# The second stage of a conv block as one fixed order of instructions, with its layer norm by transposes, bn_stats and Newton steps

## The chip, the cores and the metric

The kernel runs on one core of a Trainium2 chip. The metric is the time of one execution on the device in microseconds (us), the median over several runs. A program on one core has no second die to compare with, so a run counts as fast where it is not over 1.5% above the fastest of the same kernel. Only such runs are compared.

The engines are named as in the profile: PE (matrix products), PEld (loads of its weights, which overlap PE), DVE (vector), ACT (activation functions), POOL (general), SP (issues transfers).

## What the kernel computes

The input is sixteen images of 192 channels and 64 x 64 pixels. The part that the change touches is the second half of the block, after the batch norm's statistics are known.

```
mixed = gelu(batchnorm(mixed))                     # mixed: gated result of the first stage, in DRAM
x  = x + conv1x1(mixed, out_proj_w, out_proj_b)    # 192 -> 192
h2 = (x - mean_c(x)) / sqrt(var_c(x) + 1e-6)       # layer norm over the 192 channels (then ln2_w, ln2_b)
m  = gelu(conv1x1(h2, fc1_w, fc1_b))               # 192 -> 768
x  = x + conv1x1(m, fc2_w, fc2_b)                  # 768 -> 192
# then a depthwise 3x3 convolution whose kernel depends on the image; a mask leaves 4 taps
t    = relu(gamma * (mean_pixels(x) @ w1.T - running_mean) * rsqrt(running_var + 1e-5) + beta)
taps = (t @ w2.T + b2) * mask
out  = depthwise_conv(x, taps) + bias
```

All data is 32-bit floating point.

Of the kernel before, what the change touches and what calls it, by code (L numbers as in the profile page):

```python
"""A conv block (layer norm, gated directional scan, batch norm, MLP) followed by a
pooled dynamic depthwise convolution, on one core.

Layout. Images are taken in pairs (A, B). The 192 channels of a pair fill three tiles of 128
partitions: tile 0 is A's channels 0-127, tile 1 is B's channels 0-127, tile 2 holds channels
128-191 of A on partitions 0-63 and those of B on partitions 64-127. Per-channel constants
have two classes: class 0 for tiles 0 and 1, class 1 for tile 2.

Phase 1, per pair: layer norm, input projection, depthwise conv, four scans, local conv, gate;
the gated result goes to DRAM, its batch statistics stay on chip.  # L10
Phase 2, per pair: batch norm, gelu, output projection, layer norm, MLP; the image pair stays
in SBUF for the pooled dynamic convolution, and only its result is stored.
"""
# [8 lines left out]
F32 = mybir.dt.float32  # L22
AF = mybir.ActivationFunctionType
# [4 lines left out]
C = 192          # channels  # L28
HW = 64          # rows and columns of an image
NPIX = HW * HW  # L30
RW = HW + 2      # a padded row
CH = 512         # pixels of a chunk: 8 rows, one PSUM bank
CR = CH // HW    # rows of a chunk
NCH = NPIX // CH
GR = 2 * CR      # rows of a group of two chunks
NG = HW // GR
NFC = 6          # blocks of 128 hidden channels
LNG = 4          # chunks that share one pass of the layer norm's square root
RED = 48
NTAP = 4         # taps that the mask of the dynamic kernel lets through  # L40

# columns of the packed per-channel constants
# [6 lines left out]
def conv_block_kernel(ctx: ExitStack, tc: tile.TileContext, x, prm, w_in, w_out, w_fc1, b_fc1, w_fc2, w1, bn1, w2, out):  # L49
# [8 lines left out]
    def tiles_of(src, p, lo, hi):  # L58
        """The pieces of a pair's pixels lo..hi in DRAM: tile, partitions, source."""
        a, b = 2 * p, 2 * p + 1  # L60
        return (
            (0, slice(0, 128), src[a, 0:128, lo:hi]),
            (1, slice(0, 128), src[b, 0:128, lo:hi]),
            (2, slice(0, 64), src[a, 128:C, lo:hi]),
            (2, slice(64, 128), src[b, 128:C, lo:hi]),
        )

    def load_cls(dst, src):
        """A [192, n] array as its two classes of partitions."""
        nc.sync.dma_start(dst[:, 0], src[0:128])  # L70
        nc.sync.dma_start(dst[0:64, 1], src[128:C])
        nc.sync.dma_start(dst[64:128, 1], src[128:C])

    def pair_matmul(t, ps, w, bd, col, rhs):
        """ps = (weights' columns col.. of tile t)^T @ (the pair's 192 channels).

        w: [128, 2, n] weights by class of input channel; bd: [128, 128] its corner of class 1
        to class 1, block diagonal."""
# [10 lines left out]
    # ---------------------------------------------------------------- constants  # L89
# [14 lines left out]
    # x - mean over the channels as a matrix product  # L104
# [13 lines left out]
    def fold(w, col):  # L118
        """Scales a weight's rows (input channels) by a layer norm's weight."""
        for cls in range(2):  # L120
            nc.vector.tensor_scalar_mul(w[:, cls], w[:, cls], vec(cls, col))

    def corner(pool, name, w, col):
        """The block diagonal of a weight's class 1 inputs to its class 1 outputs."""
# [6 lines left out]
    def center(ps_tag, pool, rhs):  # L131
        """The three tiles of x - mean, in PSUM."""
# [7 lines left out]
    # ================================================================ phase 1  # L140
# [3 lines left out]
    with ExitStack() as phase:  # L144
# [4 lines left out]
        # biases of the two projections with the layer norm's bias in them  # L149
# [18 lines left out]
        # decays, and the factor mix * (1 - decay) * scale of each direction  # L168
# [21 lines left out]
        # the directions' factors as diagonals, to sum the scans in PSUM  # L190
        diag = k1.tile([128, 2, 4, 128], F32, tag="diag", name="diag")
        # the decays along padded rows, zero on the padding, where the state starts anew
# [9 lines left out]
        # the variances of LNG chunks go to 2*LNG rows of one bank; and back from there  # L202
# [13 lines left out]
        # images with a border of zeros, and the vertical scans  # L216
# [13 lines left out]
        for p in range(n_pairs):  # L230
            # ---- layer norm without its affine part
# [26 lines left out]
            for t in range(3):  # L258
                cls = t // 2
                # ---- projection and depthwise conv  # L260
# [15 lines left out]
                # ---- scans down and up, row by row  # L276
# [10 lines left out]
                # ---- scans along the rows, local conv, gate  # L287
# [33 lines left out]
        # ---- batch norm as a scale and a bias per channel  # L321
# [3 lines left out]
        # class 1: the two halves of the partitions have half of the images each  # L325
# [21 lines left out]
    # ================================================================ phase 2  # L347
# [28 lines left out]
    fold(wf1, LN2W)  # L376

    # the pair's images, with a row of zeros above and columns of zeros beside
# [7 lines left out]
    op = ctx.enter_context(tc.tile_pool(name="o2", bufs=2))  # L386
    ps2 = ctx.enter_context(tc.tile_pool(name="ps2", bufs=2, space=PSUM))

    for p in range(n_pairs):
        xi = ximg[p % n_img]  # L390
        sums = wp.tile([128, 3, NCH], F32, tag="sums", name="sums")
        for c in range(NCH):
            lo, hi = c * CH, (c + 1) * CH
            x2 = lp.tile([128, 3, CH], F32, tag="x2", name="x2")
            for t, q, src in tiles_of(xv, p, lo, hi):
                nc.sync.dma_start(x2[q, t], src)
            mx = lp.tile([128, 3, CH], F32, tag="mx2", name="mx2")
            nc.sync.dma_start(mx, mixed_d[p, :, :, lo:hi])

            # ---- batch norm, gelu, output projection, residual  # L400
            for t in range(3):
                cls = t // 2
                nc.scalar.activation(mx[:, t], mx[:, t], AF.Gelu, bias=bn_bi[:, cls:cls + 1], scale=bn_sc[:, cls:cls + 1])
            for t in range(3):
                ps = ps2.tile([128, CH], F32, tag="a", name="ps_o", bufs=3)
                pair_matmul(t, ps, wo, wo_bd, 0, lambda tt, q, mx=mx: mx[q, tt])
                nc.vector.scalar_tensor_tensor(x2[:, t], ps, vec(t // 2, OUTB), x2[:, t], ALU.add, ALU.add)  # L407

            # ---- layer norm without its affine part
            xc = center("a", ps2, lambda tt, q, x2=x2: x2[q, tt])  # L410
            sq = wp.tile([128, 3, CH], F32, tag="sq2", name="sq2", bufs=1)
            for t in range(3):
                nc.scalar.activation(sq[:, t], xc[t], AF.Square)
            h = wp.tile([128, 3, CH], F32, tag="h2", name="h2")
            rstd = []
            for i in range(2):
                q = slice(64 * i, 64 * i + 64)
                pw = ps2.tile([128, CH], F32, tag="f1", name="ps_v", bufs=2)
                nc.tensor.matmul(pw, mean_w, sq[:, i], start=True, stop=False)
                nc.tensor.matmul(pw, mean_w[q], sq[q, 2], start=False, stop=True)  # L420
                rs = wp.tile([128, CH], F32, tag="rs2", name="rs2")
                nc.scalar.activation(rs, pw, AF.Sqrt, bias=eps6)  # L422
                nc.vector.reciprocal(rs, rs)  # L423
                nc.vector.tensor_mul(h[:, i], xc[i], rs)  # L424
                nc.vector.tensor_mul(h[q, 2], xc[2][q], rs[q])

            # ---- MLP: the second product trails the first by one block of hidden channels
            po = [ps2.tile([128, CH], F32, tag="f2", name="ps_f2", bufs=3) for _ in range(3)]

            def second(m, gl, po=po):  # L430
                st, sp = m == 0, m == NFC - 1
                for i in range(2):
                    nc.tensor.matmul(po[i], wf2[:, m, 0:128], gl[:, i], start=st, stop=sp)  # L433
                for i in range(2):
                    nc.tensor.matmul(po[2][64 * i:64 * i + 64], wf2[:, m, 128:C], gl[:, i], start=st, stop=sp)  # L435

            last = None
            for m in range(NFC):
                cols = slice(128 * m, 128 * m + 128)
                gl = wp.tile([128, 2, CH], F32, tag="gl", name="gl", bufs=3)  # L440
                pf = [ps2.tile([128, CH], F32, tag="f1", name="ps_f1", bufs=2) for _ in range(2)]
                for i in range(2):
                    nc.tensor.matmul(pf[i], wf1[:, 0, cols], h[:, i], start=True, stop=False)  # L443
                for i in range(2):
                    q = slice(64 * i, 64 * i + 64)
                    nc.tensor.matmul(pf[i], wf1[q, 1, cols], h[q, 2], start=False, stop=True)  # L446
                for i in range(2):
                    nc.scalar.activation(gl[:, i], pf[i], AF.Gelu, bias=bf1[:, m:m + 1])  # L448
                if last is not None:
                    second(m - 1, last)  # L450
                last = gl
            second(NFC - 1, last)
# [85 lines left out]
```

## The kernel before

Images are taken in pairs A and B. A pair's channels fill three tiles of 128 partitions: tile 0 has A's channels 0-127, tile 1 has B's, and tile 2 has channels 128-191 of A on its lower and of B on its upper 64 partitions. The first stage (layer norm, projection, convolutions, scans, gate) is not touched. The second stage goes through the 8 pairs, and through each pair in 8 chunks of 512 pixels, 64 chunks in all. The 768 hidden channels of the MLP are 6 blocks of 128.

A product over a pair's 192 channels is split in this way, and each such product changes the shape in which PE's array is used:

```
def pair_matmul(t, ps, w, bd, col, rhs):
    if t < 2:
        hi = slice(64 * t, 64 * t + 64)
        nc.tensor.matmul(ps, w[:, 0, col:col + 128], rhs(t, slice(0, 128)), start=True, stop=False)   # "full", 128x128
        nc.tensor.matmul(ps, w[hi, 1, col:col + 128], rhs(2, hi), start=False, stop=True)             # "half", 64 rows
    else:
        nc.tensor.matmul(ps, bd, rhs(2, slice(0, 128)), start=True, stop=False)                       # block diagonal
        for i in range(2):                                                                            # "columns", 64 columns
            nc.tensor.matmul(ps[64*i:64*i+64], w[:, 0, col+128:col+C], rhs(i, slice(0, 128)), start=False, stop=True)
```

The second stage of one chunk was written straight on:

```
# ---- batch norm, gelu, output projection, residual
for t in range(3):
    nc.scalar.activation(mx[:, t], mx[:, t], AF.Gelu, bias=..., scale=...)
for t in range(3):
    ps = ps2.tile([128, CH], F32, tag="a", name="ps_o", bufs=3)
    pair_matmul(t, ps, wo, wo_bd, 0, ...)
    nc.vector.scalar_tensor_tensor(x2[:, t], ps, vec(t // 2, OUTB), x2[:, t], ALU.add, ALU.add)
# ---- layer norm without its affine part
xc = center("a", ps2, lambda tt, q, x2=x2: x2[q, tt])          # x - mean as a matrix product, 3 tiles in PSUM
for t in range(3):
    nc.scalar.activation(sq[:, t], xc[t], AF.Square)
for i in range(2):
    q = slice(64 * i, 64 * i + 64)
    pw = ps2.tile([128, CH], F32, tag="f1", name="ps_v", bufs=2)
    nc.tensor.matmul(pw, mean_w, sq[:, i], start=True, stop=False)       # variance, on all 128 partitions
    nc.tensor.matmul(pw, mean_w[q], sq[q, 2], start=False, stop=True)
    nc.scalar.activation(rs, pw, AF.Sqrt, bias=eps6)
    nc.vector.reciprocal(rs, rs)                                         # 128 x 512
    nc.vector.tensor_mul(h[:, i], xc[i], rs)
    nc.vector.tensor_mul(h[q, 2], xc[2][q], rs[q])
# ---- MLP: the second product trails the first by one block
for m in range(NFC):
    ... first product, full and half, for both images (pf, 2 banks)
    ... Gelu of both images
    if last is not None: second(m - 1, last)                             # full and columns
    last = gl
second(NFC - 1, last)
... results into the pair's image in SBUF, with their sums for the pooling
```

After a pair's eighth chunk came its pooling, its taps (matmuls with one moving column) and its convolution in 12 units, all before the next pair in the text of the program. A scheduler, not the text, settles in which order each engine takes the instructions.

## Time and profile before

| | before |
|---|---|
| median (3 runs) | 8107.52 us (8107.06 to 8109.49) |
| end of the first stage in the profile | 3864.6 us |
| first MLP product to last MLP result, 64 chunks | 3918.4 to 8029.6, 4111.2 us, 64.2 us a chunk |
| PE busy in that stretch | 3527.8 us, granted clock 0.89 |
| tail, last result to end | 78 us |

The page and the views that show this are read line by line in the prediction below. In short: in the second stage PE is the engine with the most work, and it idles in every chunk while the layer norm goes through ACT and DVE.

### The profile page before, as it was taken

How to read it: one execution, taken by the hardware profiler on the slowest of the kernel's cores; microseconds unless marked ns; L12 is line 12 of the kernel's file. 1: busy time of each engine (PE TensorE's matmuls, PEld its weight loads, DVE VectorE, ACT ScalarE, POOL GpSimd, SP SyncE). 2: the span in 40 equal slices, each digit the busy share in tenths (PEclk: the TensorE clock that was granted, in tenths of full speed). 3: DMA queues.
4: the chain of work that ended last, by engine and by line, in shares of the span. 5: the costliest groups of instructions: out<-in, count | busy, mean ns of one | idle time of the engine just before them, and what ended most of it. 6: DMA issues, size and time to landing. Idle time of an engine off the chain costs nothing.

```text
span 8107.6 us, 39958 instructions
## 1 busy us (share of the span) xinstructions
PE 6342.4 (78%) x13812; PEld 1932.3 (24%) x13812; DVE 4665.9 (58%) x6936; ACT 1722.3 (21%) x2473; POOL 150.8 (2%) x234
## 2 busy tenths in 40 slices
PE   8668686767768776755788888888888888888885
PEld 2222222222222222211222222222222222222221
DVE  4998989799898979999323224223242242322423
ACT  2112111112111111210222222222222222222222
POOL 0000000000000000000100000000000000000000
PEclk7787777778787777867798998988989889889897
DMA  1010101001010100000101011011010010100101
GB/s 49 11 51 11 34 21 42 18 13 50 11 34 24 39 18 13 34 11 34 31 24 47 31 31 50 28 32 46 24 55 24 28 52 30 55 24 24 55 24 35
DMA packets 113882, 256.48 MB, mean 32 GB/s; under 512 B 13792, under 2 KB 15072, under 8 KB 113680
## 3 DMA queue, kind: packets, MB, share of 16 engines
q1 hardware_dynamic: 85520, 153.25, 6.2%
q0 software_dynamic: 28160, 100.68, 3.4%
q8 instruction: 109, 1.79, 0.1%
q14 instruction: 93, 0.76, 0.0%
HBM read 153.21 MB, written 100.66 MB: 31 GB/s over the span
## 4 chain that ended last, share of the span: by engine, by line
PE 50%; DVE 34%; issue 9%; DMA 4%; ACT 4%; SPq 0%; POOL 0%; ACTq 0%; POOLq 0%; DVEq 0%
DVE mx L56 10%; PE ps_f L443 9%; PE ps_f L433 8%; DVE dimg L56 5%; PE ps_f L446 5%; DVE rs L423 4%; PE ps_f L435 4%; DVE bt L56 3%; DMA mx<-mixed_d 3%; DVE tb L56 3%; PE cmb L308 3%; DVE lr L301 2%; PE ps_cen L81 2%; PE pr L255 2%; PE ps_o L82 2%
## 5 line engine op out<-in xcount | busy, mean ns | idle before, releaser
L443 PE MATMUL ps_f<-h,wf 128*128 128x512 f32 x1536 | 880.4, 701 | 543.0 <-DVE h L424 518.3
L454 DVE SCALAR_TENSOR_TENSOR ximg<-ps_f,pv,x 128x512 f32<-128x512 f32 x192 | 144.4, 752 | 1898.3 <-PE ps_f L433 1875.4
L56 DVE SCALAR_TENSOR_TENSOR dimg<-pimg,pv,dimg 128x1024 f32<-128x1024 f32 x768 | 946.2, 1280 | 46.7 <-ACT dimg L272 39.2
L56 DVE SCALAR_TENSOR_TENSOR mx<-dimg,pv,mx 128x1024 f32<-128x1024 f32 x768 | 957.6, 1272 | 0.9
L448 ACT ACTIVATE gl<-ps_f,bf 128x512 f32<-128x512 f32 x768 | 485.4, 683 | 1376.2 <-PE ps_f L446 1375.5
L433 PE MATMUL ps_f<-gl,wf 128*128 128x512 f32 x1536 | 761.8, 618 | 0.0
L423 DVE RECIPROCAL rs<-rs 128x512 f32<-128x512 f32 x128 | 420.3, 3325 | 507.1 <-ACT rs L422 507.1
L308 PE MATMUL cmb<-rl,diag 128*128 128x512 f32 x384 | 260.3, 767 | 419.3 <-DVE rl L302 419.3
L443 PEld LDWEIGHTS ps_f<-h,wf 128*128 128x128 f32 x1536 | 290.4, 210 | 1089.2 <-issue 991.4
L308 PE MATMUL cmb<-lr,diag 128*128 128x512 f32 x384 | 266.5, 783 | 337.0 <-DVE lr L301 263.1
L56 DVE SCALAR_TENSOR_TENSOR bt<-bt,dec,dimg 128x64 f32<-128x64 f32 x1512 | 419.9, 278 | 158.6 <-ACT bt L283 157.9
L446 PE MATMUL ps_f<-h,wf 64*128 64x512 f32 x1536 | 477.0, 701 | 0.0
L296 ACT ACTIVATE sg<-ps_g,bi 128x512 f32<-128x512 f32 x192 | 125.2, 685 | 1610.4 <-DVE mx L315 1461.9
L56 DVE SCALAR_TENSOR_TENSOR tb<-tb,dec,dimg 128x64 f32<-128x64 f32 x1512 | 422.6, 280 | 61.7 <-ACT tb L283 61.3
L435 PE MATMUL ps_f<-gl,wf 128*64 128x512 f32 x1536 | 414.2, 618 | 0.0
L56 DVE SCALAR_TENSOR_TENSOR o<-ximg,taps,o 128x1024 f32<-128x1024 f32 x288 | 357.3, 1279 | 98.4 <-ACT o L490 95.0
L407 DVE SCALAR_TENSOR_TENSOR x<-ps_o,pv,x 128x512 f32<-128x512 f32 x192 | 143.5, 751 | 419.0 <-PE ps_o L82 328.6
L433 PEld LDWEIGHTS ps_f<-gl,wf 128*128 128x128 f32 x1536 | 260.1, 189 | 482.0 <-issue 482.0
L81 PE MATMUL ps_p<-hc,wi 128*128 128x512 f32 x256 | 199.6, 872 | 112.6 <-ACT sg L296 112.6
L255 PE MATMUL pr<-rs,spread 8*128 8x512 f32 x384 | 247.0, 774 | 39.5 <-DVE rs L250 32.3
L301 DVE TENSOR_TENSOR_SCAN lr<-dtab,dimg 128x528 f32<-128x528 f32 x192 | 240.0, 1250 | 46.7 <-PE cmb L308 46.6
L264 ACT ACTIVATE pimg<-ps_p,bi 128x512 f32<-128x512 f32 x192 | 132.6, 691 | 570.2 <-PE ps_p L82 422.4
(177 smaller groups left out, 6801.4 us busy)
## 6 DMA issues: line engine op xcount, KB each, us to landing
mixed_d<-mx POOLq DMA_DIRECT2D x96, 512.0 KB, 2.9
mx<-mixed_d SPq DMA_DIRECT2D x64, 768.0 KB, 4.9
hc<-in_x_dram SPq DMA_DIRECT2D x128, 256.0 KB, 5.2
x<-in_x_dram SPq DMA_DIRECT2D x128, 256.0 KB, 3.5
out_dram<-o POOLq DMA_DIRECT2D x64, 512.0 KB, 2.9
hc<-in_x_dram SPq DMA_DIRECT2D x128, 128.0 KB, 5.2
x<-in_x_dram SPq DMA_DIRECT2D x128, 128.0 KB, 3.7
out_dram<-o POOLq DMA_DIRECT2D x64, 256.0 KB, 3.4
```

What stands on the lines that cost most here:

```text
L56: nc.vector.scalar_tensor_tensor(o, in0, scalar, in1, ALU.mult, ALU.add, **kw)
L81: nc.tensor.matmul(ps, w[:, 0, col:col + 128], rhs(t, slice(0, 128)), start=True, stop=False)
L82: nc.tensor.matmul(ps, w[hi, 1, col:col + 128], rhs(2, hi), start=False, stop=True)
L255: nc.tensor.matmul(pr, spread[:, j, t], rs, start=True, stop=True)
L301: nc.vector.tensor_tensor_scan(lr, dtab[:, cls, 0], row, 0.0, ALU.mult, ALU.add)
L308: nc.tensor.matmul(dst, diag[:, cls, k], src, start=(k == 0), stop=(k == 3))
L423: nc.vector.reciprocal(rs, rs)
L433: nc.tensor.matmul(po[i], wf2[:, m, 0:128], gl[:, i], start=st, stop=sp)
L435: nc.tensor.matmul(po[2][64 * i:64 * i + 64], wf2[:, m, 128:C], gl[:, i], start=st, stop=sp)
L443: nc.tensor.matmul(pf[i], wf1[:, 0, cols], h[:, i], start=True, stop=False)
L446: nc.tensor.matmul(pf[i], wf1[q, 1, cols], h[q, 2], start=False, stop=True)
L448: nc.scalar.activation(gl[:, i], pf[i], AF.Gelu, bias=bf1[:, m:m + 1])
```

## The change

The intent has two parts that do not depend on each other.

**The layer norm.** Each quarter of a chunk is transposed by PE so that pixels lie on the partitions. DVE's bn_stats then gives mean and variance of 192 channels in one instruction per image. The inverse root is taken on 128 x 8 numbers by DVE alone, from an integer shift as a first guess and three Newton steps, so ACT needs no Sqrt. Transposes of the broadcast result spread it back over the channels. The mean is not subtracted from the data at all: `W (x - mean) = (W - its mean over the input channels) x`, so the centring matrix goes into the MLP's first weight, once.

**The order.** The second stage is written as one fixed program, kept in the order of its text (`manual_schedule`). While the six MLP blocks of a chunk run, the next chunk's output projection, statistics and normalisation, and the last pair's convolution, are put into the blocks at fixed places, each product beside others of its own shape.

The core of the diff; "..." marks cuts, and "[before]" and "[after]" say from which kernel a passage is.

```
+        fold(wf1, LN2W)                     # [after] ln2_w into the weight, then the mean out of it
+        for j in range(2):
+            ...
+                pair_matmul(t, ps, cen, cen_bd, 0, lambda tt, q, cs=cs: wf1[q, tt // 2, cs])
+        ...                                  # copied back into wf1

-            xc = center("a", ps2, ...)       # [before]
-            ... Square, variance products, Sqrt, reciprocal, multiplies
+        def pixels(self, j):
+            pt = bank("ps_x")
+            for n, t in enumerate((0, 2, 1)):
+                nc.tensor.transpose(pt[:, 128*n:128*n+128], self.x2[:, t, cols], ident)
+        def moments(self, j):
+            for i in range(2):
+                nc.vector.bn_stats(self.stats[:, j, i], self.pt[j][:, i * C:(i + 1) * C])
+        def rstd(self):                      # 4 small instructions for the variance v, then
+            nc.vector.tensor_scalar(yi, vi, 1, None, ALU.logical_shift_right)
+            nc.vector.tensor_scalar(yi, yi, -1, 0x5f3759df, ALU.mult, ALU.add)
+            for _ in range(3):
+                nc.vector.tensor_mul(u, y, y)
+                nc.vector.scalar_tensor_tensor(u, u, -0.5, v, ALU.mult, ALU.mult)
+                nc.vector.scalar_tensor_tensor(y, u, 1.5, y, ALU.add, ALU.mult)
+        def spread(self, i):
+            for j in range(NB):
+                nc.tensor.transpose(self.pr[i][:, 128*j:128*j+128], self.y[:, n:n+1].broadcast_to([128, 128]), ident)
+        def norm(self, i):
+            nc.vector.tensor_mul(self.h[:, i], self.x2[:, i], self.pr[i])
+            nc.vector.tensor_mul(self.h[q, 2], self.x2[q, 2], self.pr[i][q])

+    with tc.manual_schedule():
+        ... front of chunk 0, bare
+        for k in range(n_chunks):
+            for m in range(NFC):
+                ... loads of chunk k+2 (m = 1); end of a convolution unit of the last pair
+                ... MLP first product, full                          (cur, block m)
+                if m == 1: nxt.out01_full()                          # next chunk, in its own shape
+                elif m == 2: nxt.out2_full()
+                elif m == 3: nxt.pixels(0), moments(0), pixels(1), moments(1)
+                elif m == 4: nxt.spread(0); nxt.norm(0)
+                second_full(*trail)                                  # block m-1
+                if m == 3: nxt.pixels(2), moments(2), pixels(3), moments(3); nxt.rstd()
+                elif m == 4: nxt.spread(1); nxt.norm(1)
+                ... MLP first product, half; Gelu; nxt.out01_half (m = 1)
+                second_cols(*trail); nxt.out2_cols (m = 2); nxt.gelu (m = 0)
+                ... begin of a convolution unit of the last pair
```

The convolution's units were halved (one chunk's rows instead of two), with four output buffers instead of two.

## The prediction

> **What bounds the kernel now.** I read the slices of the span first, to find the stages:
>
> ```profile
> PE   8668686767768776755788888888888888888885
> DVE  4998989799898979999323224223242242322423
> PEclk7787777778787777867798998988989889889897
> ```
>
> The span breaks near the middle. In the left half DVE is full (9s) and PE waits on it: that is the first stage, which the change leaves alone. In the right half PE is at 8, DVE at 2 to 3, and the granted clock dips again and again below full speed. The timeline puts the last first-stage instruction at 3864.6 us, the first second-stage matmul at 3888.1, the last result of the 64 chunks at 8029.6, and the end at 8107.6. So 8029.6 - 3888.1 = 4141.5 us go to 64 chunks, 64.7 us each. Only this part is at stake.
>
> Next, busy time in one ordinary chunk (from one RECIPROCAL to that of the next chunk; columns: window, length, busy of PE, PEld, DVE, ACT, POOL, granted clock, DMA share, GB/s):
>
> ```profile
> 4616.36:4677.91 61.55, 53.70 (x132) 16.11 (x132) 13.52 (x15) 15.23 (x23) 0.00 (x0) 0.92 0.08 26
> ```
>
> PE is busy 53.7 of 61.55 us, everything else a quarter or less: a PE-bound stage with a hole of some 8 us in each chunk. The chain of waits shows what is in the hole (start, length, what):
>
> ```profile
> 5059.99 1.91 PE ps_f L433 x4
> 5061.91 1.01 PE ps_f L435 x4
> 5062.92 1.05 PE ps_o L81 x2
> 5063.97 1.05 PE ps_o L82 x2
> ...
> 5069.28 4.83 DMA mx<-mixed_d
> ...
> 5076.85 0.52 ACT L422
> 5077.36 0.78 issue
> 5078.14 0.70 ACT rs L422
> 5078.84 0.02 issue
> 5078.86 6.56 DVE rs L423 x2
> 5085.43 0.56 DVE h L424
> 5085.98 0.14 issue
> 5086.12 3.75 PE ps_f L443 x4
> 5089.87 1.06 PE ps_f L446 x4
> ...
> 5093.04 1.98 PE ps_f L443 x4
> ```
>
> From the last output projection (5069.2) to the first MLP product (5086.1) the path runs through the load of the next gated image, which ACT needs for work queued ahead of the layer norm's; the ACT table load and Sqrt (L422); and two RECIPROCALs of 3.3 us. Meanwhile PE does the centring and variance products and then idles. The waits view says how long:
>
> ```profile
> PE ps_f L443 <- DVE h L424: 486.7, 60, 13.5
> ```
>
> that is 8.1 us per chunk. The last chain lines show a second charge: the first L443 group after the hole takes 3.75 us, the same group later 1.98.
>
> A third loss is at each pair's end. At 4388.98 us pooling begins, and the next MLP product starts at 4438.88: 50 us, where the ordinary gap from last MLP product to first is 5005.4 to 5024.9, 19.5 us. In between, DVE's convolution work (L56) stands ahead of the next RECIPROCAL. 30 us x 7 boundaries = 210 us, so 64 x 61.4 + 210 = 4140, which closes the account.
>
> **What the Trainium skill says.** "TensorE: Matmul & The Clock Gate", part 1 (What's actually happening): PE runs at half clock after about 3.4 us of idling and needs about as long to recover. The trace agrees: 3.75 against 1.98 us after the hole. "ScalarE: Activation LUTs", What ACT_TABLE_LOAD costs: some 1.28 us per table load. The trace has 1283 ns, at two functions, Sqrt and Gelu, per chunk. "VectorE: DVE Perf Modes", First, the fixed hardware budget: Reciprocal runs an iterated divide with a repeat count of 8. The trace has 3344 ns for 512 elements, against 0.65 us for a multiply of the same shape. The TensorE page, part 4 (PE-mode transpose), gives some 275 ns for a 128x128 bf16 transpose inside a kernel. The kernel before has none, so no run yet confirms it, least of all for 32-bit data.
>
> **The change, part by part.** Prices of PE work come from the chain: a lone matmul 1.05 us, two of one shape 1.91, so 0.86 for each further one and about 0.19 when the tile shape of the array changes (128x128, two 64-row halves side by side, two 64-column halves side by side). A side-by-side pair costs as one: 1.06 and 1.01.
>
> *Removed.* Centring (1.91+1.06+1.06+1.03 = 5.1 us) and variance products (4 x 1.05 = 4.2 us) of PE; Square, Sqrt and both table loads on ACT; both RECIPROCALs on DVE; the 8.1 us wait; the cold restart (3.75 - 1.91, some 1.8 us); 30 us at each boundary.
>
> *MLP.* 24 full products, 6 pairs of halves and 6 of columns are 36 units, 36 x 0.86 = 31.0. Before, each of six blocks changed shape four times (1.91+1.06+1.91+1.01 = 5.89, so 35.3 per chunk). Now the second product's full part follows the first's, and the next chunk's output projection goes into groups of its own shape, so three changes: 6 x 3 x 0.19 = 3.4. Sum 34.4.
>
> *Output projection.* 2 full, one pair, one block diagonal, one column pair: 5 x 0.86 = 4.3 with no extra shape change (before 6.3).
>
> *Added on PE.* 12 transposes to pixels and 8 to spread the result: 20 x 0.275 = 5.5 by the skill's figure. For a floor, the N=1 matmuls L475 show a pair of 128-column weight loads in 0.31 us warm, 0.155 each. If each 32-bit transpose is two instructions it could be 0.35 to 0.4. So 3.1 to 8.
>
> *Pooling.* Its small matmuls now stand in the stream of PE: about 5 us per pair by the warm rows (16 of 0.31 or 0.20, four of 0.19), 0.6 per chunk.
>
> *Beside PE.* DVE per chunk: six results and residuals at 0.75, 8 bn_stats (678 ns for 512 elements, so about 0.3 for 192), 15 tiny operations at 0.2 (rows of 0.15 to 0.17), 4 multiplies at 0.65, and 3 convolution units of 3 x 0.75: 4.5+2.4+3.0+2.6+6.8 = 19.3 us, under half of a chunk. ACT: 12 Gelu at 0.68, 3 at 0.8, 3 convolution starts at 0.75: 13 us. Both hide. The tight place is block 3 to 4: after the last pixels, PE has halves, columns and the next full group, about 1.05+1.05+1.9 = 4 us, and DVE in that time two or so bn_stats and the 15-step chain, 0.7+3.0. It just fits; I allow 0.3 us.
>
> Sum per chunk: 34.4+4.3+5.5+0.6+0.3 = 45.1, against 64.7. 64 x 45.1 = 2886 us.
>
> *Ends.* Before the loop, folding the mean into the weight adds 10 cold matmuls and four copies, about 10 us; the first chunk's front is bare (output projection about 12 us cold, transposes and statistics 6, chain 3, spread and norm 5): first MLP product at about 3925, against 3918.4 before. The tail was 78 us: 46 of DVE, the rest waits for two output buffers. Now 8 of pooling, 24 x 3 x 0.75 = 54 of DVE, and about 11 from last store to end as now: 75.
>
> Total 3925 + 2886 - 5 (the last chunk has no follower) + 75 = 6881 us.
>
> **Rivals.** (a) *Transposes cost more than thought*: two passes, or a drained array at each of the four switches. For: 32-bit data, no trace of them here. 0.4 each adds 2.5 us per chunk, 160 us: about 7040. At 0.155 each: about 6730. (b) *A new wait takes the hole's place*: DVE's strict order puts convolution work or the 15-step chain before what PE needs, and PE idles in block 4. For: the slack is under 1 us. Against: DVE is under half loaded and PE has another block to run after the norm. If the small steps take 0.3 instead of 0.2, PE idles 1 to 2 us per chunk: 6950 to 7000. If gaps also drop the clock it could reach 7150. (c) *DVE or DMA becomes the bound*: 19 of 45 us and a DMA share of 0.08 to 0.13 speak against it; loads run a whole chunk ahead. This would need 60 us per chunk to leave the time unchanged. (d) *The hole was hidden anyway*: no, PE is the engine waiting.
>
> **Range and chances.** The transpose price moves the total by -150 to +160, the wait by 0 to +120, and the ends by 15. I say 6880 us, 6710 to 7080 in 8 of 10. For less than 2% gain (7945) a chunk would have to cost 62 us: faster 0.97, same 0.02, slower 0.01.
>
> **What would show it.** Right: PE above 9 in the right half's slices, clock near full there, chunk period 43 to 47 us, no table loads and no RECIPROCAL of 128x512, the wait of the MLP's first product on h gone, DVE near 4 tenths, transposes near 0.2 to 0.35 us apart. Wrong: a PE wait on the Newton chain (y) or on banks of the transposes, or transposes well off 0.275 us.

## The result

| | before | after |
|---|---|---|
| median | 8107.33 us (8107.06 to 8109.49, 4 runs) | 6641.55 us (6638.98 to 6644.0, 4 runs) |
| ratio of the fast runs | 1 | 0.8195 (95%: 0.8184 to 0.8207) |
| end of the first stage in the profile | 3864.6 us | 3854.6 us |
| first MLP product to last MLP result | 3918.4 to 8029.6 us | 3903.9 to 6562.3 us |
| an ordinary chunk | 61.55 us | 40.80 us |
| tail | 78 us | 74.9 us |

A ratio here is worked out from the fast runs of both kernels; it is not quite the ratio of the two medians (0.8192). The change takes 18% off. The direction and the place were as predicted, and the time lies 68 us below the range of 6710 to 7080 us.

The slices of the span of the kernel after (40 equal slices, busy share or granted clock in tenths):

```profile
PE   8848678678678678677665569999999999999995
DVE  3898997998998987998999952353435353535355
PEclk8877787687787787777867779999999999999997
```

From slice 24 on PE shows nines without a dip, and so does its clock. The windows view gives the same as numbers. Its columns are window, length, then busy time (and instructions) of PE, PEld, DVE, ACT and POOL, then granted clock, DMA share and GB/s. First the second stage of the kernel before:

```profile
3918.40:8029.60 4111.20, 3527.76 (x8692) 1081.92 (x8692) 1175.36 (x1263) 1064.98 (x1476) 61.24 (x112) 0.89 0.11 35
```

and the same stage after, with one ordinary chunk below it:

```profile
3903.90:6562.30 2658.40, 2657.43 (x8567) 1031.71 (x8566) 1124.45 (x2837) 736.25 (x1125) 122.70 (x224) 0.99 0.16 53
5044.24:5085.04 40.80, 40.80 (x131) 15.55 (x131) 20.59 (x48) 12.50 (x19) 3.27 (x6) 1.00 0.21 65
```

PE is busy in 2657.43 of 2658.40 us. So of 583 us of idle time (4111.20 - 3527.76) all but 1 us went, and 870 us of PE's own busy time (3527.76 - 2657.43), 13.6 us a chunk. Of these, an estimate from the rows of both chains accounts for some 12: the centring and variance products, 9.3, less 2.3 for transposes, 1.1 and 2.0 in the MLP and the projection from fewer changes of shape, and 1.8 from the slow restart. The rest is not separated. Next to nothing is left to wait for in this stage: it is almost exactly as long as PE's work.

In an ordinary chunk the chain of waits of the kernel after is therefore a list of PE groups and nothing else. Its columns are start, length and what ran; these are the two blocks of one chunk that hold the transposes:

```profile
5044.24 1.91 PE ps_f L617 x4
5046.15 0.66 PE ps_x L459 x6
5046.81 1.72 PE ps_f L581 x4
5048.52 0.66 PE ps_x L459 x6
5049.18 1.06 PE ps_f L652 x4
5050.24 1.01 PE ps_f L585 x4
5051.25 1.91 PE ps_f L617 x4
5053.16 0.56 PE ps_r L491 x4
5053.72 1.72 PE ps_f L581 x4
5055.44 0.44 PE ps_r L491 x4
```

L617 and L652 are the full and half part of the MLP's first product, L581 and L585 the full part and the columns of the second. L459 are the transposes to pixels and L491 those that spread the result. Two products show as x4, so a 32-bit product is two instructions; six transposes show as x6, so a transpose is one. The instructions of a chunk's transposes take 0.66 + 0.66 + 0.56 + 0.44 = 2.32 us of PE's stream, where the prediction had 5.5. The L617 group takes 1.91 us in every ordinary chunk; none is at the 3.75 us of a restart.

One transpose by itself looks quite different. The view of line L459 has, for one instruction, shortest, median and longest duration in ns:

```profile
L459 PEld LDWEIGHTS ps_x<-ident,x x768: 138/141/143, 3895.1 to 6509.6; 128*128 128x128 f32 x192
L459 PE MATMUL ps_x<-ident,x x768: 272/273/329, 3895.1 to 6509.7; 128*128 128x128 f32 x192
```

A transpose is 273 ns from its start to its end, and six of them in a row are done in 0.66 us, 110 ns each, because the next starts long before the last has ended. That is most of the miss (204 of 244 us), as the experiments and the account below show.

At the tight place, between statistics and spreading, the timeline of the kernel after (start, length, engine, line, operation) has the end of the Newton chain and the first spreading transposes of one chunk:

```profile
5134.38 0.17 DVE L481 SCALAR_TENSOR_TENSOR ny<-nu,ny 128x8 f32<-128x8 f32 x1
5134.69 0.62 PE L491 MATMUL ps_r<-ident,ny 128*128 128x128 f32 x4
```

The chain ends at 5134.55 us and PE takes the result at 5134.69. These 0.14 us look like slack, but they are not. The same gap stands in the bare front of the first chunk, where PE has nothing else to do (from the chain of waits):

```profile
3901.73 0.18 DVE ny L481
3901.91 0.14 issue
3902.04 1.94 PE ps_r L491 x8
```

It is 0.14 or 0.15 us in all chunks but those in which the taps stand before the spreading. So 0.14 us is what the hand-over from DVE to PE takes, and PE is already waiting. How long can be read from the chunk above: four spreading transposes take 0.56 us behind the Newton chain and 0.44 us in the next group. PE loses some 0.12 us in each of 56 chunks, about 7 us in all. The waits view does not show it.

At a pair's boundary, PE runs the taps, matmuls with a single moving column, in its stream. The chain there shows this (of the 16 pieces of taps only the last two are shown):

```profile
4263.95 0.31 PE ps_k L527 x2
4264.26 0.20 PE ps_k L528 x2
4264.46 1.01 PE ps_r L491 x4
4265.47 2.98 PE ps_f L581 x4
```

The 16 pieces take 4.1 us from 4260.36 on. After them four transposes take 1.01 us instead of 0.56 and four instructions of L581 2.98 instead of 1.72. The windows view (columns as above) has the granted clock at 1.00 during the taps and at 0.57 after them, though PE counts as busy throughout:

```profile
4260.36:4264.46 4.10, 4.10 (x34) 3.86 (x34) 0.00 (x0) 0.00 (x0) 0.00 (x0) 1.00 0.00 0
4264.46:4268.44 3.98, 3.98 (x10) 2.12 (x11) 1.57 (x5) 0.00 (x0) 0.00 (x0) 0.57 0.00 0
```

The taps thus cost their own time and, at this boundary, some 1.7 us of slower clock after it. Over the seven boundaries a slower clock follows at six (at the one of 4593 us it stays at 1.00), and at the last four it begins during the taps and costs some 3 us.

### The profile page after: what moved, and what is told of

The parts are those of the page before. It is cut to its first block, busy times and chain, and to the rows that moved or that the text cites. A ratio compares the mean times of both kernels' runs of the same rounds, so it can differ in the third digit from the quotient of the medians.

```text
span 6637.2 us, 41594 instructions
## 1 busy us (share of the span) xinstructions
PE 5460.5 (82%) x13704; PEld 1882.0 (28%) x13704; DVE 4621.9 (70%) x8572; ACT 1388.3 (21%) x2121; POOL 221.0 (3%) x362
## 4 chain that ended last, share of the span: by engine, by line
PE 62%; DVE 34%; issue 2%; ACT 1%; DMA 0%; SPq 0%; ACTq 0%; POOL 0%; POOLq 0%; DVEq 0%
DVE mx L57 12%; PE ps_f L617 11%; PE ps_f L581 10%; DVE dimg L57 6%; PE ps_f L652 6%; PE ps_f L585 6%; DVE bt L57 4%; DVE tb L57 4%; PE cmb L309 4%; DVE lr L302 2%; PE ps_cen L82 2%; PE ps_cen L83 2%; PE pvar L246 2%; PE pr L256 2%; DVE rl L303 2%
## 5 line engine op out<-in xcount | busy, mean ns | idle before, releaser
L617 PE MATMUL ps_f<-h,wf 128*128 128x512 f32 x1536 | 762.8, 619 | 0.0
L581 PE MATMUL ps_f<-gl,wf 128*128 128x512 f32 x1536 | 731.7, 599 | 0.0
L57 DVE SCALAR_TENSOR_TENSOR o<-ximg,taps,o 128x512 f32<-128x512 f32 x576 | 430.6, 751 | 172.2 <-ACT o L541 158.0
L652 PE MATMUL ps_f<-h,wf 64*128 64x512 f32 x1536 | 433.5, 641 | 0.0
L585 PE MATMUL ps_f<-gl,wf 128*64 128x512 f32 x1536 | 414.2, 618 | 0.0
L617 PEld LDWEIGHTS ps_f<-h,wf 128*128 128x128 f32 x1536 | 260.5, 189 | 495.5 <-issue 422.9
L581 PEld LDWEIGHTS ps_f<-gl,wf 128*128 128x128 f32 x1536 | 284.8, 192 | 310.4 <-issue 309.4
L464 DVE BATCH_NORM_STATS2 stats<-ps_x 128x6 f32<-128x192 f32 x512 | 148.1, 352 | 170.5 <-PE ps_x L459 170.5
L242 ACT ACTIVATE hc<-ps_cen 128x512 f32<-128x512 f32 x192 | 117.0, 609 | 636.8 <-PE ps_cen L87 636.8
```

The costliest lines, as they stand in the source:

```text
L57: nc.vector.scalar_tensor_tensor(o, in0, scalar, in1, ALU.mult, ALU.add, **kw)
L464: nc.vector.bn_stats(self.stats[:, j, i], self.pt[j][:, i * C:(i + 1) * C])
L581: nc.tensor.matmul(f.pf2[i], wf2[:, m, 0:128], gl[:, i], start=(m == 0), stop=(m == NFC - 1))
L585: nc.tensor.matmul(f.pf2[2][64 * i:64 * i + 64], wf2[:, m, 128:C], gl[:, i], start=(m == 0), stop=(m == NFC - 1))
L617: nc.tensor.matmul(pf[i], wf1[:, 0, cols], cur.h[:, i], start=True, stop=False)
L652: nc.tensor.matmul(pf[i], wf1[q, 1, cols], cur.h[q, 2], start=False, stop=True)
```

## The experiments

Twelve runs were made, all correct: eleven further kernels and the kernel after once more. Small effects are read from the second stage in the trace (first MLP product to last MLP result), because the end of the untouched first stage varies between 3854.6 and 3882.1 us over the profiles of these runs, whatever the kernel. Why it does is open. That stage is 2658.4 us long in the kernel after, and 2661.4 us in its repeat on the second chip.

| kernel | median, us | ratio to before (95%) | second stage, us | against after, us a chunk |
|---|---|---|---|---|
| after | 6641.55 | 0.8195 (0.8184 to 0.8207) | 2658.4 | |
| t_twice | 6790.27 | 0.837 (0.835 to 0.839) | 2789.6 | +2.05 |
| t_matmul | 6796.16 | 0.838 (0.8362 to 0.8397) | 2795.5 | +2.14 |
| newton6 | 6744.98 | 0.8319 (0.8301 to 0.8337) | 2760.2 | +1.59 |
| sqrt | 6712.41 | 0.8275 (0.8255 to 0.8295) | 2720.4 | +0.97 |
| ln_only | 7597.69 | 0.9381 (0.9365 to 0.9397) | 3609 | +14.9 |
| order_only | 6998.29 | 0.864 (0.8627 to 0.8653) | 3022 | +5.7 |
| shapes | 6697.27 | 0.8269 (0.8257 to 0.8281) | 2711.5 | +0.83 |
| auto | 6664.81 | 0.8228 (0.8216 to 0.824) | 2689.5 | +0.49 |
| border | 6636.17 | 0.8198 (0.8187 to 0.8209) | 2661.4 | +0.05 |
| best | 6662.12 | 0.8226 (0.8215 to 0.8237) | 2691.1 | +0.51 |
| after_again | 6644.48 | 0.8202 (0.8191 to 0.8214) | 2661.4 | +0.05 |
| best2 | 6566.92 | 0.8107 (0.8095 to 0.8119) | 2615.6 | -0.67 |

The theory was that the transposes had been priced at their duration instead of at their spacing in PE's stream. Rivals were that the time below the prediction came from elsewhere (fewer shape changes than thought, a hole with more in it), with transposes that partly hide.

### What a transpose costs: t_twice and t_matmul

The first kernel issues each transpose twice, to the same place.

```
-  nc.tensor.transpose(pt[...], self.x2[:, t, cols], ident)
+  nc.tensor.transpose(pt[...], self.x2[:, t, cols], ident)
+  nc.tensor.transpose(pt[...], self.x2[:, t, cols], ident)      # and the same in spread()
```

Expected:

> The changed kernel with each of its 20 transposes per chunk issued twice, to the same place. Theory: a transpose takes its place in the stream of PE for 0.11 us (0.66 us for six in the chain of waits), so a chunk grows by 20 x 0.11 to 0.12 = 2.2 to 2.4 us and the kernel from 6641 to about 6790 us. Rival 1, the price of the prediction (0.275 us each): plus 352 us, about 6990. Rival 2, transposes lie in the shadow of something else: about 6641, no change.

Measured: 6790.27 us. The stage grew by 131 us, 2.05 us for 20 further transposes in a chunk, 0.10 us each. With the further work PE no longer waits the 0.12 us for the Newton chain (eight spreading transposes take 0.87 us in a row, 5056.19 to 5057.06), and with this counted it is 0.11 each. The row of a single one still says 273 ns. At the price of the prediction the time would have been near 6990 us. So the marginal cost of a transpose is its spacing, and the duration in the row is not spent by PE.

The second kernel writes the same operation as an ordinary product with the identity.

```
-  nc.tensor.transpose(o, in, ident)
+  nc.tensor.matmul(o, in, ident, start=True, stop=True)
```

> The changed kernel with the 20 transposes written as plain 32-bit products with the identity. Theory: what makes the transpose cheap is that it is one instruction; a plain product is two, each with its own weight load, so 0.22 to 0.31 us instead of 0.11: 2.2 to 4 us per chunk more, 6780 to 6900 us in all, which is about the price that the prediction used. Rival: a product of 128 columns costs the same as the transpose, 6641 us.

Measured: 6796.16 us, at the low end. The chain of this kernel:

```profile
5036.93 1.34 PE ps_x L459 x12
5038.27 1.72 PE ps_f L582 x4
5039.99 1.34 PE ps_x L459 x12
```

Six products are now twelve instructions of 0.11 us, so 0.22 us each. Hence a transpose is cheap twice over: it is a single instruction where a 32-bit product is two, and each instruction moves 128 columns, where one of 512 columns takes 0.43 us (1.72 / 4). The spacing of 0.11 us is a quarter of that.

### The tight place: newton6 and sqrt

The first kernel has three Newton steps more than needed, nine small DVE instructions, some 1.8 us at their spacing of 0.2 us. PE's work stays the same.

```
-  for _ in range(3):
+  for _ in range(6):
```

> The changed kernel with six Newton steps instead of three: nine more tiny DVE operations of 0.2 us, 1.8 us, on the chain from the last bn_stats to the first spreading transpose. Theory: in the trace the chain ends 0.1 us before PE wants it, so nearly all of it becomes a wait of PE: about 1.7 us x 64 = 109 us more, 6750 us. Rival: PE has other work queued and the chain is hidden, 6641 us.

Measured: 6744.98 us, the stage 102 us longer. The waits view (engine, what it waited for, us in total, times, longest):

```profile
PE ps_r L491 <- DVE ny L481: 102.8, 57, 5.5
```

The longest, 5.5 us, lies in the bare front before the stage. The other 56 make 97.3 us of the 102 us, so the stage grew by 1.8 us in each of 56 chunks, which is all of the added work. At the seven boundaries nothing is added, because there PE does the taps between statistics and spreading. The average of 1.59 us a chunk in the table mixes the two. So the change has no slack at this place in an ordinary chunk, as the 0.14 us of the hand-over showed.

The second kernel takes the root on ACT again, on 128 x 8 numbers, with a reciprocal of the same size on DVE.

```
-  shift, first guess, 3 Newton steps
+  nc.scalar.activation(y, v, AF.Sqrt)
+  nc.vector.reciprocal(y, y)
```

> The changed kernel with Sqrt on ACT and a reciprocal of 8 columns in place of shift and Newton steps. Theory: the DVE chain loses 11 operations (2.2 us), but ACT loads a table twice per chunk (2 x 1.28 us) and, as it takes its work in order, holds the Gelu of block 3 back until the statistics are there; PE then waits for that Gelu in block 4: 0.5 to 1.5 us per chunk, 6670 to 6740 us. Rival: at 12.5 us busy of 41 ACT has room for both loads, 6641 us or a little less.

Measured: 6712.41 us, the stage 62 us longer. A line of its waits, then four of its chain:

```profile
PE ps_f L612 <- ACT gl L649: 46.0, 63, 0.7
```

```profile
5020.55 1.28 ACT L649
...
5021.85 0.70 ACT gl L649
...
5022.59 1.13 PE ps_f L612 x2
5023.72 0.44 PE ps_r L486 x4
```

The chain itself became shorter, but ACT has to load a table (1.28 us) for Sqrt and another to come back to Gelu, and PE waits for the Gelu behind it, 0.7 us a chunk, 46 of the 62 us. The rest is not separated; the two products behind the wait take 1.13 us where 0.86 is usual. The last line shows the other side: with the shorter chain the first spreading group takes 0.44 us and not 0.56. In sum the Newton steps are worth 1.0 us a chunk against Sqrt at this place in ACT's order.

### The two parts alone: ln_only and order_only

The first is the kernel before with the new layer norm in the old place; the scheduler orders it.

```
+  fold of the mean into wf1
-  center, Square, variance products, Sqrt, reciprocal, multiplies
+  transposes, bn_stats, Newton steps, spreading transposes, multiplies    # straight on, in the old place
```

> The kernel before with the new layer norm (transposes, bn_stats, Newton steps, mean folded into the weight) in its old program order, scheduled as before; the pipeline is left out. Theory: the hole between last output projection and first MLP product shrinks from 16.9 us to about 8.5 (residual 0.9, transposes and statistics 3, chain 3, spread and multiply 1.8), the chunk from 61 to about 53 us, and the 30 us at each pair's end stay: about 7550 us, 7400 to 7650. Rival: the layer norm's cost was the whole hole and the order adds nothing, then about 6650 to 6900.

Measured: 7597.69 us, 502 us less than before on the same chip (8099.49 us). Its waits view, and its chain from the end of the output projection (start, length, what):

```profile
PE ps_r L454 <- DVE ny L447: 346.0, 64, 17.3
```

```profile
5071.37 1.03 PE ps_o L87 x4
...
5073.71 2.22 DVE stats L434 x8
...
5078.66 0.18 DVE ny L447
...
5078.98 1.94 PE ps_r L454 x8
5080.91 3.71 PE ps_f L474 x4
```

From 5072.40 to the first MLP product at 5080.91 are 8.5 us, in which PE mostly waits for the statistics and the Newton chain, in every one of the 64 chunks, and then restarts at 3.71 us instead of 1.91. A lighter layer norm in the old place saves PE's work and leaves a hole.

The second has the new order with the old layer norm.

```
-  pixels, moments, rstd, spread, norm in blocks 3 and 4; fold of the mean
+  out projection in blocks 0-1; center in block 2; ACT copies x - mean and its square to SBUF;
+  variance products in block 3, then Sqrt and the 128x512 reciprocals; gelu of the chunk ahead in block 5
```

> The changed kernel's fixed order with the old layer norm (centring and variance products on PE, Square, Sqrt and two table loads on ACT, two RECIPROCALs of 3.3 us on DVE), its steps spread over the blocks so that each has time; the centred tiles are copied out of PSUM by ACT. Theory: no wait is left, PE does 34.2 + 4.3 + 4.3 (centring) + 2.6 (variance) = 45.4 us per chunk: about 6940 us. So the order alone would be worth some 1170 of the 1466 us, and the new layer norm in it some 300. Rival: the 6.6 us of RECIPROCALs and the table loads come back as waits, over 7100.

Measured: 6998.29 us, 1101 us less than before, and 58 us more than expected. A line of its waits, and the piece of its chain that it comes from:

```profile
PE ps_f L599 <- ACT gl L622: 69.2, 63, 1.1
```

```profile
5025.32 1.28 ACT L622
```

PE waits 1.1 us a chunk for a Gelu behind a table load, 69 us in all; the expectation missed that, and in size this accounts for the 58 us.

The four corners, on the same chip:

| | old order | fixed order |
|---|---|---|
| old layer norm | 8099 | 6998 (-1101) |
| new layer norm | 7598 (-502) | 6644 (-1455, after_again) |

The order is the larger part. ("Fixed order" holds here all that order_only shares with the change, the halved convolution units and the four output buffers too; no run takes these apart.) Both together give 148 us less than the sum of the parts. One reason can be read from the rows: the centring and variance products that the new layer norm removes cost 9.3 us a chunk in the old order, but only 8 x 0.86 = 6.9 in the fixed order, where they stand beside products of their own shape (the variance products take 1.72 + 0.86 us in the chain of order_only, 4.2 before). Taking them out and putting in transposes of 2.3 us saves 6.9 - 2.3 = 4.6 us, and the wait of 1.1 us goes too: 5.7 us, and the table above has 5.7. That the hole is removed only once counts as well; the runs do not separate the two.

### Changes of the array's shape: shapes

In four of the six blocks the second product's full part is moved behind the first product's halves, as before the change, so that each of these blocks changes shape four times instead of three.

```
-  if trail: second_full(*trail)                     # right after the first product's full part
+  if trail and m in (3, 4): second_full(*trail)
   ... first product, half; Gelu
+  if trail and m not in (3, 4): second_full(*trail)
```

> The changed kernel with the second product's full part moved behind the 64-row halves in four of six blocks, so that PE changes its tile shape four times instead of three in these blocks; the work is the same. Theory: each change costs 0.19 us, 4 x 0.19 = 0.76 us per chunk, about 6690 us. Rival: the gaps come from waits and not from the change of shape, 6641 us.

Measured: 6697.27 us, the stage 53 us longer, 0.83 us a chunk, 0.21 us for each of four changes. The chain:

```profile
5012.13 1.06 PE ps_f L652 x4
5013.19 1.91 PE ps_f L581 x4
```

L581 after another shape takes 1.91 us instead of 1.72. The prediction's 0.19 us for a change of shape holds, and this rival explains none of the miss.

### Is it the fixed order, or the text: auto

The text stays, but the scheduler may reorder it.

```
-  with tc.manual_schedule():
+  if True:
```

> The changed kernel with the same statements but without the fixed schedule, so that the scheduler orders each engine's instructions. Theory: the gain comes from the places of the work in the order of PE, DVE and ACT, so a different order lets waits back in: 6700 to 7200 us. Rival: the statements' own order and contents are enough and the scheduler keeps close to them, 6641 us.

Measured: 6664.81 us, the stage only 31 us longer. The theory that the fixed order by itself is needed missed; the rival, that the scheduler keeps close to the order of the statements, was nearly right. Its largest wait of PE in the second stage is small:

```profile
PE ps_x L459 <- DVE x L449: 10.2, 8, 1.4
```

So almost all of the gain lies in how the stage is written (the next chunk's work named inside this chunk's blocks), and some 20 us (0.3%, against after_again on the same chip) in forbidding the scheduler to move it.

### The start of the stage, and versions that go further: border, best, best2

Between the batch norm's last constant and the first MLP product lie 49.3 us in the kernel after. The view of two lines, one row each (shortest, median and longest duration in ns, first and last start):

```profile
L129 DVE COPY wo_bd<-wo x2: 192/9572/18953, 3857.5 to 3876.5; 64x64 f32<-64x64 f32 x2
L397 POOL MEMSET ximg<- x2: 10823/10823/10823, 3854.8 to 3865.6; 128x12870 f32 x2
```

A copy of 64 x 64 numbers on DVE takes 18.95 us. It begins while POOL clears the two whole images (10.8 us each) and ends with the second of them. Only the border of the images has to be zero:

```
-  nc.gpsimd.memset(xi, 0.0)
+  nc.gpsimd.memset(xi[:, :, 0:1], 0.0)
+  nc.gpsimd.memset(xi[:, :, :, 0:1], 0.0)
+  nc.gpsimd.memset(xi[:, :, :, RW - 1:RW], 0.0)
```

> The changed kernel with only the borders of the two image buffers set to zero instead of the whole of them. In the trace of the changed kernel a DVE copy lasts 19 us while GpSimd clears the buffers, and the second stage begins behind it. Theory: the start of the second stage comes some 18 to 20 us earlier, about 6621 us. Rival: the weights' loads are the bound there and it is under 8 us.

Measured: 6636.17 us. The copy in that kernel:

```profile
L129 DVE COPY wo_bd<-wo x2: 186/189/192, 3860.0 to 3860.5; 64x64 f32<-64x64 f32 x2
```

The start is 39.3 us, 10 less and not the 19 expected: with the copy out of the way, the load of the MLP weights (until 3863.3 us), the bias products and the cold products of the fold set the time. In the total the gain cannot be told from none, as the ratio intervals of border and after overlap.

The kernel best adds to it that the columns of the second product run for two blocks at once, in every other block, to save shape changes.

```
-  second_cols(*trail)                       # each block
+  if trail and m % 2 == 0:
+      second_cols(*older); second_cols(*trail)
```

> As the run with the borders alone, and the 64-column parts of the second product of two blocks done together in every other block, which takes away one of three changes of tile shape in every other block. Theory: 3 x 0.16 us per chunk, 31 us in all, on top of the 20 of the borders: about 6590 us. Rival: a change of shape costs nothing by itself, then as the run with the borders alone.

Measured: 6662.12 us, 18 us slower than after_again on the same chip rather than some 50 faster. Its waits view says why:

```profile
PE ps_r L493 <- DVE ny L483: 54.1, 57, 3.7
```

3.7 us of it lie before the stage, so it is 0.9 us in each of 56 chunks. The columns that ran in block 3 had stood between the statistics and the spreading. Moving them away took 1 us out of PE's work at just the place without slack, so PE waited for the Newton chain. A saving of PE time became a wait.

The kernel best2 keeps the columns in block 3 and gathers others.

```
+  if trail and m in (0, 2, 3, 5):
+      if m in (2, 5): second_cols(*older)
+      second_cols(*trail)
+  # the taps of tiles 0 and 1: one matmul for both images, two moving columns
+  nc.tensor.matmul(pk[:, k:k + NTAP + 1:NTAP], w2t[:, k, 0:128], self.red, start=True, stop=True)
+  # the last pair's tail: PE convolves tile 1 by four diagonal products a chunk, ACT adds the bias; DVE tiles 0 and 2
+  # and the border of zeros as in border
```

> The changed kernel with four edits: only the image borders set to zero (10 us by the trace of the run with the borders alone); the 64-column parts of the second product gathered in four places of a chunk instead of six, none of them taken from between statistics and spreading (two changes of shape at 0.16 to 0.19 us less per chunk, 20 to 24 us); the kernel taps of both images in one product (about 1.5 us per pair, 12 us); and in the last pair's convolution one of three tiles by diagonal products on PE, so that DVE has 16 units of 2.25 us instead of 24 (18 us). Theory: about 60 us in all, 6580 us. Rival: as in the run that gathered the columns before, a wait on the Newton chain eats the gain: 6620 us or more.

The kernel after ran again beside it, to have both from one chip and the same rounds:

> The changed kernel as it is, on the same chip and in the same rounds as the next kernel, for a fair comparison: 6640 us, within 10 us.

Measured: 6566.92 us against 6644.48 us for after_again, 77.6 us or 1.2% less. Its second stage and its tail in the windows view (columns as above):

```profile
3893.90:6509.40 2615.50, 2614.56 (x8511) 1016.94 (x8510) 1123.93 (x2836) 736.76 (x1125) 123.04 (x224) 1.00 0.17 54
6509.40:6565.10 55.70, 34.58 (x96) 16.89 (x96) 37.14 (x62) 17.41 (x24) 17.53 (x32) 0.76 0.37 113
```

The stage is 46 us shorter than in after_again with no wait of PE in the view (2614.56 busy of 2615.50), the start 10 and the tail 19 us. Of the 46, the ordinary chunk gives 16 (40.54 us instead of 40.80). The boundaries give 29: there the chunks take 25.4 us beyond ordinary ones in sum, where they take 54.7 in after_again. The taps last 2.1 us instead of 4.1, and a slower clock follows them at two boundaries, where it follows at all seven in after_again. This is more than twice the 12 us expected of the taps. This version is faster than both kernels.

## Why the prediction was wrong, and where it was right

The direction, the place (the stage's hole and its boundaries) and the mechanism were right. The time predicted is 6881 us, and the profiled execution took 6637.2, 244 us less. Along the prediction's own sum:

| term | predicted | measured | difference, us |
|---|---|---|---|
| first stage's end | 3864.6 | 3854.6, within what runs vary | -10 |
| from there to the first MLP product | 60.4 (3925) | 49.3 (3903.9) | -11 |
| transposes, a chunk | 5.5 | 2.32 | -3.18 x 64 = -204 |
| wait allowed for, a chunk | 0.3 | 0.12, already in the 2.32 | -19 |
| MLP, a chunk | 34.4 | 6 x (1.91 + 1.72 + 1.06 + 1.01) = 34.2 | -13 |
| output projection, a chunk | 4.3 | 1.72 + 0.86 + 0.86 + 0.86 = 4.3 | 0 |
| pooling, all boundaries | 38 | about 51 | about +13 |
| last result to end | 75 | 74.9 | 0 |

The terms of the loop add up to -223, and the loop was 223 us shorter than predicted. One slip of the sum changes nothing: the parts of the tail, 8 + 54 + 11, make 73 and not 75.

**The step that failed** is "20 x 0.275 = 5.5 by the skill's figure". It took the duration of one transpose for the time that one takes in PE's stream. The figure as such is right here: the Trainium skill, "TensorE: Matmul & The Clock Gate", part 4 (PE-mode transpose), gives about 275 ns in a kernel's context, there for 16-bit data (bf16), and the trace has 273. But PE starts the next one 0.11 us later, and t_twice shows that a further one costs 0.10 to 0.11. So the term is 2.3 us a chunk and not 5.5, which is 204 of the 244 us. The same page, part 2 (Back-to-back issue gap), has a sustained spacing of about 81 ns for matmuls of 128 columns, and says that this is what matters for throughput. That is not 110 ns, but it is the right kind of number, and the prediction passed it over. It could also have been had from the profile of before without any page: 0.86 us for a product of 512 columns in two instructions is 0.43 us each, and a quarter of the columns is 0.11.

**The floor failed too.** The 0.155 us read from the taps' rows was no lower limit for a weight load: the taps' pairs alternate between 128 and 64 columns of the array, so these rows probably carry part of the 0.19 us of a shape change (no run separates it). With a false floor of 3.1 us under the term, rival (a) was bounded at 6730 and the range at 6710, and the measured 2.32 us lies below both. Rival (a) named the right term. Its title and its first case look to the wrong side, as the transposes cost less and not more, and its cheap case stops at the false floor.

**Right:** PE's nines and a clock near full in the second half; the wait of the first product on the layer norm gone; the shape change of 0.19 us (shapes: 0.21); the projection's 4.3 us; DVE's load of 19.3 us a chunk (20.59 measured) beside PE; the tail. In the second stage of the trace of the kernel after no table load is left but the one before its first Gelu, and no RECIPROCAL of 128 x 512. The tight place was named and the 0.3 us allowed for it was enough: PE waits 0.12 us there in an ordinary chunk. It does not fit with room to spare, and newton6 and best each paid at once for what they added or moved.

**Off, but small:** the taps were priced at their warm rows, about 5 us a pair, without the clock that falls after them at six of seven boundaries; and the first chunk's front took 14.7 us (3889.2 to 3903.9) instead of 26: its output projection was done in 5.9 us (until 3895.1) instead of 12, and spreading took 1.9 instead of 5.

Two of its own signs of being right failed with the same term: the chunk takes 40.80 us and not 43 to 47, and the transposes are 0.11 us apart and not 0.2 to 0.35.

**Rivals (b) and (c)** did not come in the size that they named: PE waits 0.12 us a chunk for the Newton chain and not 1 to 2, and DVE is busy 1124 of 2658 us, with the DMA share at 0.16.

**Open:** why the end of the first stage varies by some 27 us between runs of the same instructions; what decides whether the clock falls after the taps; and whether the spacing of 0.11 us is set by the 128 columns moved or by the load of a new weight for each transpose, as both are of the same size here.

## What to carry to other kernels

Price an instruction of a full stream by the spacing of a run of them, from a chain row such as "x6 in 0.66 us", or by scaling a known row to its number of moving columns; the duration of one instruction is for a lone step on a dependent path. Where one engine carries a stage, the largest gain here was in writing the next step's work into the present step's blocks: the order alone gave 1101 us, the cheaper layer norm alone 502. Once such a pipeline has no slack, a saving at the wrong place turns into a wait, so look at what stands between a chain's start and its end before moving anything out of there. A small constant gap between the end of a chain and the start of what needs it is not slack by itself: compare it with a place where the engine is known to wait.

## What the Trainium skill lacked or had wrong

- "TensorE: Matmul & The Clock Gate", part 4 (PE-mode transpose): only the duration of one transpose stands there, about 275 ns, which this trace confirms (273 ns). What a stream of them costs is lacking: 0.11 us each for 128 x 128 of 32-bit data, with 0.10 to 0.11 us for each further one in t_twice. It is also lacking that such a transpose is one instruction, where a 32-bit product with the identity is two (0.22 us in t_matmul). The page's Terms say of the transpose mode that it is four times faster for FP32, without saying than what; here it is twice as fast as that product.
- The same page, part 2 (Back-to-back issue gap): its spacings of 81 ns for 128 columns and 131 ns for 512 name no data type. In this case's 32-bit products an instruction of 512 columns takes 0.43 us, and a product is two, 0.86 us.
- The same page, part 3 (Packing small matmuls): it says that weight loads overlap running matmuls only where the row group differs, though its text above that line also names a background weight buffer. Here the loads of the L581 group, 128 x 128 after 128 x 128, hide: four instructions take 1.72 us with a load of 0.19 us for each. What is exposed is a change of the array's shape, 0.19 us in the rows and 0.21 us in the run shapes, which no page gives in time. ("TensorEngine Tiling (Array Packing)", Key Properties, says only that changing the tiling mode drains the engine.)
- No page gives what a row of matmuls with one moving column does to the clock: PE counts as busy through 16 pieces in 4.1 us here, and the granted clock is 0.57 in the 4 us after them, with the next group at 2.98 us instead of 1.72. It varies: the clock fell at six of seven boundaries in after and at all seven in after_again, and at two of seven in best2, where the taps take 2.1 us. That the taps set it off is inferred from these three traces; no run tested it alone.
